# A gated attention and mixture block: batch 1's keys ahead of its transposes, an earlier table load, and a fourth weight base summed early

## The chip, the cores and the metric

The kernel runs on one core of a Trainium2 chip. The metric is the device time of one execution in microseconds (us), as the median of several runs. A core has five engines that each work through a program of their own in order: TensorE (PE, with its weight loads shown apart as PEld), VectorE (DVE), ScalarE (ACT), GpSimd (POOL) and SyncE (SP). They wait for each other by semaphores. SP, ACT and POOL also issue DMAs, and an issue stands in the engine's program like any other instruction.

## The reference

Eight batches of 256 tokens of width 512, all in float32. Cut to what matters:

```python
def attend(x, ctx):                       # x normed; 32 query heads, 8 key heads of 16
    q = heads(concat(ctx, x) @ Wq)
    k = concat(rep(heads(ctx @ Wsk)), rep(heads(x @ Wk)))     # along the keys
    v = concat(rep(heads(ctx @ Wsv)), rep(heads(x @ Wv)))
    s = q @ k.T / 4 + alibi               # only the last 64 positions of each half are seen
    return softmax(s) @ v @ Wo

def ffn(x):                               # x normed
    p4, i4 = top_k(softmax(x @ w_router), 4)
    basis = silu(x @ w_gate) * (x @ w_up)                     # 8 bases of 256 columns
    mixed = sum over the 4 of p4/sum(p4) * scale[i4] * mix[i4] over the bases
    return mixed @ w_down + (silu(x @ sg) * (x @ su)) @ sd    # a shared part of 512

x = x + tanh(g_xattn) * attend(layernorm(x), ctx)
x = x + tanh(g_ffn) * ffn(layernorm(x))
```

## The kernel before

Tokens are handled in two tiles of 128. Each batch b passes through four generators: `project(b)` (norm, transposes, keys, queries, values), `attention(b)` (scores, softmax, value products), two `tail(b, t)` (out-projection, residual, second norm, router) and `feed_forward(b)`.

**Order by hand.** The program runs under a manual schedule: what the Python code emits first stands first on its engine. `run` (L1212) holds the live generators with a virtual time each and always steps the one that is earliest; a generator yields a number of units, and its `start` call says how long all its units are in batches (one batch is about 117 us). So a yield moves no instruction by itself. It decides what is written between two instructions.

**The prologue.** Batch 0's inputs and the attention weights are loaded by SP and ACT (L127 to L145). 14 transposes of an identity (`WARM`, L169) keep PE busy until data arrive. `project_first` (L374) computes batch 0's keys of the context, the transposes of tile 0, the first half of four query groups (the half over the context), then tile 1's transposes, tile 0's keys and the second halves. ACT's first computing instruction (L168) brings in its table; it stands behind all of ACT's load issues.

**The first softmax.** `first_batch` (L728) goes through 19 steps u. A step softens one block of 4 head pairs on DVE (L641), takes exponentials on ACT (L660), divides the block before on POOL (L672) and transposes the one before that on DVE (L685); every second step has new scores on PE (L628), and steps 6, 10, 14 and 18 have value products on PE (L707). Between these, `piece` lets the generator `rest` go on by one slot: a yield of BEFORE or MORE means that the next slot is PE work, AFTER that it is an eviction. `rest` (L437) does batch 0's values, tile 1's keys and queries, and then all of `project(1)`: transposes of tile 0, of tile 1 (L531), the context keys and the keys (L543), four query groups in two halves each (L562), the values (L582). What is left when the steps are over goes on in `others` (L486).

**PSUM banks.** Four banks hold scores, one has the tag "one", three are the gate banks gu0 to gu2. `own` in `rest` takes gu2 and "one" in turn, beginning with gu2; all of `project(1)` is in "one", so each product there waits until the one before has been evicted.

**The bases.** The feed-forward uses sums of weight quarters. The first time that a base k (0 to 9, two of them shared) is used, four sums (`sub`, L947, L953) are made in place and stored to scratch in DRAM (`keep`, L955, L957); later batches load them. `first_weights` (L269) does this for bases 2, 0 and 1 during the first softmax, with all sums on POOL; its loads stand on SP. From base 3 on, `feed_forward(0)` makes the sums of base k during piece k - 1, two on DVE and two on POOL, and stores them between that piece's end and piece k (L1095 to L1133). Each quarter has two buffers, so base k + 2 is loaded when piece k is done with its own (`after`, L357); a base that is already summed (`summed`) takes two loads where another takes one, for three of its four quarters.

**Attention's other parts.** `diagonals` (L491) copies batch values into block form with 16 DMAs per batch, on SP for batches from 1 on.

Of the kernel before, what the change touches and what calls it, by code (L numbers as in the profile page):

```python
# [15 lines left out]
P = 128  # L16
# [14 lines left out]
NSI = SI // P  # L31
LN_EPS, EPS = 1e-5, 1e-8
MASKED = 1e32
WARM = 14


@with_exitstack
def gated_block(
# [44 lines left out]
    def next_bank(name):  # L83
        turns[0] += 1
        return ps_gu.tile([P, 2, T], F32, tag=f"gu{turns[0] % 3}", name=name)
# [24 lines left out]
    def load(b, eng=nc.sync):  # L110
        xt = three.tile([P, NT, HID], F32, tag="x", name=f"x_{b}")
        eng.dma_start(xt, x[b].rearrange("(t p) d -> p t d", p=P))
        return xt
# [7 lines left out]
    def weight(src, rows, cols, name, eng):  # L121
        t = const.tile([P, rows // P, cols], F32, tag=name, name=name)
        eng.dma_start(t, src.rearrange("(c p) n -> p c n", p=P))
        return t
# [8 lines left out]
    def load_queries(half):  # L133
        nc.scalar.dma_start(
            wq_sb[:, half * NC : (half + 1) * NC, :],
            wq[half * HID : (half + 1) * HID].rearrange("(c p) n -> p c n", p=P),
        )
# [1 line left out]
    load_queries(0)  # L139
    wk_sb = weight(wk, HID, HK * D, "wk", nc.scalar)  # L140
    nc.scalar.dma_start(x_0[:, 1, :], x[0, P:, :])
    load_queries(1)
    wsv_sb = weight(wsv, HID, HK * D, "wsv", nc.scalar)
    wv_sb = weight(wv, HID, HK * D, "wv", nc.scalar)
    loaded[1] = load(1, nc.scalar), load_context(1, nc.scalar)  # L145

    ident = const.tile([P, P], F32, tag="ident", name="ident")
    make_identity(nc, ident)
# [17 lines left out]

    warm = const.tile([P, 1], F32, tag="warm", name="warm")
    nc.scalar.activation(warm, neghalf[:, :1], AF.Tanh)  # L168
    idle = next_bank("idle")  # L169
    for _ in range(WARM):  # L170
        nc.tensor.transpose(idle[:, 0, :P], ident, ident)
# [96 lines left out]

    def first_weights():  # L269

        for k in (2, 0, 1):
            for g in range(1, 5):
                load_gu(k, g)
            if k == 2:
                yield 2.0
                later["wd"] = weight(w_down, I, HID, "wd", nc.sync)


                later["sd"] = sd = const.tile([P, NSI // 2, HID], F32, tag="sd", name="sd")
                nc.sync.dma_start(  # L280
                    sd, sw_down.rearrange("(j o p) n -> o p j n", o=2, p=P)[1]
                )
            if k == 0:
                yield 5.5
                yield from first_sums(2)
        yield 1.0
        yield from first_sums(0)
        yield 1.0
        yield from first_sums(1)
# [84 lines left out]
    def project_first():  # L374

        xt, ctT = loaded[0]
        xnT = two.tile([P, NC, T], F32, tag="xo", name="xnT_0")
        kT = two.tile([P, 2, 2, T], F32, tag="kT", name="kT_0")
        qT = two.tile([P, NB, G, Q], F32, tag="qT", name="qT_0")
        tiles = [slice(t * P, (t + 1) * P) for t in range(NT)]  # L380

        def early(name, parts):
            bank = ps_sc.tile([P, 512], F32, tag="sc", name=name)
            return bank.rearrange("p (a n) -> p a n", a=parts)

# [13 lines left out]

        def queries(pq, g, cols, cs):  # L400
            for c in cs:
                nc.tensor.matmul(  # L402
                    pq, lhsT=wq_sb[:, c, g * P : (g + 1) * P],
                    rhs=(ctT if c < NC else xnT)[:, c % NC, cols],
                    start=(c == 0), stop=(c == 2 * NC - 1),
                )

        def put_queries(pq, g, t):
            blocks = slice(t * NB // NT, (t + 1) * NB // NT)
            nc.scalar.activation(  # L410
                qT[:, blocks, g, :], pq.rearrange("p (b q) -> p b q", q=Q), AF.Copy, scale=-0.25
            )

        def two_tiles(shape, name):
            return next_bank(name).rearrange("p t (a n) -> p (t a) n", n=P)

        pk = early("pk_0", 2)
        keys(pk, 0, slice(0, T))
        evict = transposed(xnT, first_normed[0], 0, "x0", lambda shape, name: early(name, NC))
        pqs = [next_bank(f"pq_0_{g}")[:, 0, :P] for g in range(G - 1)]  # L420
        pqs.append(ps_one.tile([P, P], F32, tag="one", name="pq_0_3"))
        for g in range(G):
            queries(pqs[g], g, tiles[0], range(NC))
        put_keys(pk, 0, slice(0, T))
        evict()
        evict = transposed(xnT, first_normed[1], 1, "x0", lambda shape, name: early(name, NC))
        keys(pk, 1, tiles[0])
        for g in range(G):
            queries(pqs[g], g, tiles[0], range(NC, 2 * NC))
        put_keys(pk, 1, tiles[0])  # L430
        evict()
        for g in range(G):
            put_queries(pqs[g], g, 0)
        projected[0] = kT, qT


        def rest():  # L437
            banks = [0]

            def own(name):  # L440
                banks[0] += 1
                if banks[0] % 2:
                    return other_bank(2, name)
                return ps_one.tile([P, 2 * T], F32, tag="one", name=name)

            pv = own("pv_0").rearrange("p (t s n) -> p t s n", t=NT, s=2)
            for t in range(NT):
                yield BEFORE if t == 0 else MORE
                for s, (w_sb, src) in enumerate(((wsv_sb, ctT), (wv_sb, xnT))):
                    for c in range(NC):  # L450
                        nc.tensor.matmul(
                            pv[:, t, s, :], lhsT=src[:, c, tiles[t]], rhs=w_sb[:, c, :],
                            start=(c == 0), stop=(c == NC - 1),
                        )
            yield AFTER
            put_values(pv)
            for qd, eng in enumerate((nc.sync, nc.gpsimd, nc.sync, nc.gpsimd)):
                diagonals(qd, eng)
            yield BEFORE
            pk = own("pk_0_1").rearrange("p (s n) -> p s n", s=2)  # L460
            keys(pk, 1, tiles[1])
            yield AFTER
            put_keys(pk, 1, tiles[1])
            normed = norm(loaded[1][0], range(NT), "a1")
            for g in range(G):
                yield BEFORE
                pq = own(f"pq_0_{g}_1")[:, :P]
                queries(pq, g, tiles[1], range(2 * NC))
                yield AFTER
                put_queries(pq, g, 1)  # L470
                if g == 1:
                    xns = normed()
            ready.add("queries")
            yield from project(1, xns)

        fill.append(rest())
        fill.append(next(fill[0]))
# [29 lines left out]
    def project(b, xns=None):  # L507
# [16 lines left out]
            xns = normed()  # L524
            yield 3.0
        xnT = two.tile([P, NC, T], F32, tag="xo", name=f"xnT_{b}")
        if b == 1:
            yield BEFORE
        for t in range(NT):
            yield from own()  # L530
            evict = transposed(xnT, xns[t], t, f"x{b}", bank)  # L531
            yield AFTER
            evict()
            free()
            yield BEFORE


        kT = two.tile([P, 2, 2, T], F32, tag="kT", name=f"kT_{b}")
        yield from own()
        pk = bank([P, 2, T], f"pk_{b}")  # L540
        for s, (w_sb, src) in enumerate(((wsk_sb, ctT), (wk_sb, xnT))):
            for c in range(NC):
                nc.tensor.matmul(  # L543
                    pk[:, s, :], lhsT=w_sb[:, c, :], rhs=src[:, c, :],
                    start=(c == 0), stop=(c == NC - 1),
                )
            yield AFTER if s else MORE
        for par in range(2):
            for s in range(2):
                nc.scalar.activation(  # L550
# [1 line left out]
                )  # L552
        free()
        yield BEFORE


        qT = two.tile([P, NB, G, Q], F32, tag="qT", name=f"qT_{b}")
# [414 lines left out]
    def feed_forward(b):  # L972
# [120 lines left out]


        for k in range(PIECES):  # L1095
            late = b == 0 and k > 2
            more = b == 0 and 2 < k + 1 < PIECES
            if k == NK:
                shT = one.tile([P, NSI, T], F32, tag="shT", name=f"shT_{b}")
            one_and_five(k)  # L1100
# [125 lines left out]
    project_first()  # L1226
    start(attention(0), 0.38, at=-0.585, total=70.0)
    start(after_diagonals(), 0.2, at=-0.535, total=1.0)
    start(first_weights(), 0.39, at=-0.537, total=20.5)
    start(attention(1), 0.86, at=FIRST, total=74.1)  # L1230
    at = -0.2
    while 0 not in sides:
# [52 lines left out]
```

## Time and profile before

| | |
|---|---|
| runs | 1024.79, 1022.11, 1021.71 us |
| median | 1022.11 us |
| profiled execution | 1024.93 us, of which the span of its instructions 1023.2 us |
| mean granted TensorE clock | 0.991 |
| busy: PE, PEld, DVE, ACT, POOL | 988.1, 797.4, 602.4, 443.5, 470.7 us |
| first score product of batch 0 | 18.49 us |
| first gate product of batch 0 (L1001) | 97.04 us |
| DMA | 192.15 MB, mean 188 GB/s |

The profile is of one execution. Times in it are counted from the start of the span. An engine is busy while it computes; the issue of DMAs is not counted. Where an engine stood idle, the trace names what ended the idle time. "DMA share" is the mean busy share of the core's 16 DMA engines; the granted clock is that of TensorE as a share of full speed.

### The profile page before, as it was taken

How to read it: one execution, taken by the hardware profiler on the slowest of the kernel's cores; microseconds unless marked ns; L12 is line 12 of the kernel's file. 1: busy time of each engine (PE TensorE's matmuls, PEld its weight loads, DVE VectorE, ACT ScalarE, POOL GpSimd, SP SyncE). 2: the span in 40 equal slices, each digit the busy share in tenths (PEclk: the TensorE clock that was granted, in tenths of full speed). 3: DMA queues.
4: the chain of work that ended last, by engine and by line, in shares of the span. 5: the costliest groups of instructions: out<-in, count | busy, mean ns of one | idle time of the engine just before them, and what ended most of it. 6: DMA issues, size and time to landing. Idle time of an engine off the chain costs nothing.

```text
span 1023.2 us, 27845 instructions
## 1 busy us (share of the span) xinstructions
PE 988.1 (97%) x10470; PEld 797.4 (78%) x10470; DVE 602.4 (59%) x2241; ACT 443.5 (43%) x1657; POOL 470.7 (46%) x892
## 2 busy tenths in 40 slices
PE   8788799899999999999999999999999999999998
PEld 8666687777888788886778868787787868786885
DVE  2664766667563775536755377545766466765453
ACT  3653553336542464425643255433654245442231
POOL 4763676635543265423634236432455335651341
PEclk9899899999999999999999999999999999999999
DMA  6933754479444793547844586445954468664891
GB/s 209 246 125 96 235 163 148 156 214 293 155 144 145 198 306 124 165 147 209 268 145 146 166 220 235 136 155 178 279 183 138 145 189 258 202 196 158 270 308 60
DMA packets 117302, 192.15 MB, mean 188 GB/s; under 512 B 12848, under 2 KB 34864, under 8 KB 117168
## 3 DMA queue, kind: packets, MB, share of 16 engines
q1 hardware_dynamic: 112672, 184.87, 58.3%
q10 hardware_dynamic: 4112, 4.46, 1.3%
q8 instruction: 83, 1.36, 0.5%
q0 software_dynamic: 384, 1.05, 0.5%
q14 instruction: 51, 0.42, 0.1%
HBM read 158.87 MB, written 14.68 MB: 170 GB/s over the span
## 4 chain that ended last, share of the span: by engine, by line
PE 82%; DVE 9%; issue 3%; ACT 3%; POOL 2%; DMA 1%; SPq 1%; ACTq 0%; DVEq 0%; POOLq 0%
PE m L1001 34%; PE m L1010 10%; PE pq L562 8%; PE sc L707 6%; PE po L866 5%; PE sc L628 4%; PE pd L1144 4%; PE pk L543 3%; PE pv L582 2%; PE pd L1147 2%; DVE pr L641 1%; ACT pr L660 1%; PE pq L402 1%; PE pl L896 1%; DVE th L968 1%
## 5 line engine op out<-in xcount | busy, mean ns | idle before, releaser
L672 POOL TENSOR_SCALAR pr<-pr,rd 128x192 f32<-128x192 f32 (+2 forms) x512 | 211.1, 430 | 250.2 <-DVE rd L669 231.6
L660 ACT ACTIVATE pr<-pr,nm 128x192 f32<-128x192 f32 (+2 forms) x512 | 220.0, 433 | 112.6 <-DVE nm L641 59.9
L1001 PE MATMUL m<-w,sT 128*128 128x256 f32 x1024 | 252.5, 380 | 0.9 <-issue 0.6
L1001 PEld LDWEIGHTS m<-w,sT 128*128 128x128 f32 x1024 | 193.7, 190 | 28.8 <-issue 1.5
L641 DVE CUSTOM_DVE_ANT_1 pr<-sc,nbias 128x192 f32<-128x192 f32 (+2 forms) x512 | 154.0, 322 | 101.6 <-PE sc L628 95.4
L1001 PE MATMUL m<-w,hT 128*128 128x256 f32 x768 | 203.9, 388 | 1.0 <-DVE u L1046 1.0
L1001 PEld LDWEIGHTS m<-w,hT 128*128 128x128 f32 x768 | 139.6, 191 | 25.6 <-issue 6.5
L1091 POOL TENSOR_TENSOR mixed<-mixed,th 128x256 f32<-128x256 f32 x112 | 81.3, 726 | 139.3 <-DVE th L1086 139.3
L685 DVE STREAM_TRANSPOSE pt<-pr 128x768 f32<-128x768 f32 (+2 forms) x128 | 111.5, 871 | 4.6 <-POOL pr L672 3.1
L660 ACT ACTIVATION_READ_ACCUMULATOR pr<-pr,nm 128x1 f32 x512 | 98.5, 192 | 0.0
L1047 POOL TENSOR_TENSOR m<-m,u 128x256 f32<-128x256 f32 x80 | 61.3, 766 | 69.1 <-DVE u L1046 60.2
L963 ACT ACTIVATE th<-m 128x256 f32<-128x256 f32 x80 | 30.8, 385 | 138.3 <-DVE up L1057 138.2
L707 PEld LDWEIGHTS sc<-pt,vbd 64*32 64x32 f32 x5120 | 61.3, 107 | 26.1 <-issue 14.1
L707 PE MATMUL sc<-pt,vbd 64*32 64x64 f32 (+2 forms) x5120 | 69.1, 230 | 9.0 <-DVE nm L641 5.2
L1069 DVE TENSOR_TENSOR gate<-u,m 128x256 f32<-128x256 f32 x80 | 33.3, 416 | 70.1 <-PE m L1001 66.3
L1057 DVE TENSOR_TENSOR up<-u,m 128x256 f32<-128x256 f32 x80 | 33.3, 417 | 67.9 <-PE m L1001 41.0
L628 PE MATMUL sc<-kT,qT 32*128 32x192 f32 (+2 forms) x1024 | 64.6, 337 | 4.6 <-DVE nm L641 4.2
L628 PEld LDWEIGHTS sc<-kT,qT 32*128 32x128 f32 x1024 | 44.8, 185 | 28.7 <-issue 8.9
L963 ACT ACTIVATE th<-gate 128x256 f32<-128x256 f32 x80 | 33.2, 416 | 76.4 <-DVE gate L1069 76.4
L1010 PE MATMUL m<-sT,w 128*128 128x128 f32 x512 | 66.0, 278 | 0.0
L1010 PEld LDWEIGHTS m<-sT,w 128*128 128x128 f32 x512 | 62.3, 194 | 0.4
L1144 PE MATMUL pd<-sd,shT 128*128 128x512 f32 x128 | 61.5, 603 | 0.1
(131 smaller groups left out, 1375.9 us busy)
## 6 DMA issues: line engine op xcount, KB each, us to landing
w<-s SPq DMA_DIRECT2D x284, 256.0 KB, 3.5
w<-in_L_ffn_w_gate SPq DMA_DIRECT2D x130, 256.0 KB, 3.0
w<-in_L_ffn_w_up SPq DMA_DIRECT2D x73, 256.0 KB, 4.1
vbd<-vpad SPq DMA_DIRECT2D x120, 128.0 KB, 3.0
s<-w SPq DMA_DIRECT2D x40, 256.0 KB, 3.2
w<-in_L_ffn_shared_w_gate SPq DMA_DIRECT2D x32, 256.0 KB, 2.7
w<-in_L_ffn_shared_w_up SPq DMA_DIRECT2D x18, 256.0 KB, 3.8
sd<-in_L_ffn_shared_w_down SPq DMA_DIRECT2D x16, 256.0 KB, 3.5
```

What stands on the lines that cost most here:

```text
L562: nc.tensor.matmul(pq, lhsT=wq_sb[:, c, g * P : (g + 1) * P], rhs=(ctT if c < NC else xnT)[:, c % NC, :], start=(c == 0), stop=(c == 2 * N ...
L628: nc.tensor.matmul(seen(scs[p][:, j * COLS : (j + 1) * COLS], qb), lhsT=qT[rows, qb].rearrange("p g q -> p (g q)"), rhs=kT[rows, par, :, f ...
L641: nc.vector.tensor_tensor_reduce(out=part, in0=seen(scs[p][:, j * COLS : (j + 1) * COLS], qb0 + j), in1=bass.AP(tensor=bias.tensor, offset ...
L660: nc.scalar.activation(part, part, AF.Exp, bias=nmax, scale=-1.0, accum_out=den)
L672: nc.gpsimd.tensor_scalar(part, part, rden[:, p : p + 1], 1.0, op0=ALU.mult, op1=ALU.mult)
L685: nc.vector.transpose(pt[:, u % 4].rearrange("p c (s k) -> p (c s) k", s=2)[:, :, lo:], pr.rearrange("p c (s k) -> p (c s) k", s=2)[:, :, ...
L707: nc.tensor.matmul(scs[gp][32 * c : 32 * (c + 1), 2 * COLS + lo * Q : 2 * COLS + hi * Q], lhsT=vbd[rows, kb % (P // Q), kb // (P // Q) * 2 ...
L963: nc.scalar.activation(th, gate, AF.Tanh, scale=0.5)
L1001: nc.tensor.matmul(dst, lhsT=sides_of[m][c], rhs=w[:, c, :], start=(first and c == 0), stop=(c == NC // 2 - 1), skip_group_check=True,)
L1010: nc.tensor.matmul(dst[:, cols], lhsT=w[:, c, cols], rhs=sides_of[m][c], start=(first and ic == c == 0), stop=(c == NC // 2 - 1), skip_gro ...
L1091: nc.gpsimd.tensor_add(mixed[t], mixed[t], th)
L1144: nc.tensor.matmul(po, lhsT=shT[:, ic, t * P : (t + 1) * P], rhs=down[ic], **flags)
```

## The change

- `WARM` is 20 instead of 14.
- ACT's table load comes ahead of the loads of the second half of wq, of wsv and of wv; batch 1's inputs are loaded by ACT after the first eviction of transposes.
- In `project_first` tile 0's transposes stand between the second and the third query group.
- `own` in `rest` begins with "one".
- `project(1)` does the context keys first (in "one"), then both transposes (in gu2), then the other keys, and has one empty slot ahead of its queries. From batch 2 on, 1.0 unit is added after each eviction of transposes.
- `first_weights` handles bases 2, 3, 0, 1. Base 3's sums follow base 2's; bases 0 and 1 are loaded after that. Its length and units go from 0.39 and 20.5 to 0.40 and 25.5. `feed_forward(0)` makes sums only for bases from 4 on.

```diff
-WARM = 14
+WARM = 20
...
     nc.scalar.dma_start(x_0[:, 1, :], x[0, P:, :])
-    load_queries(1)
-    wsv_sb = weight(wsv, HID, HK * D, "wsv", nc.scalar)
-    wv_sb = weight(wv, HID, HK * D, "wv", nc.scalar)
-    loaded[1] = load(1, nc.scalar), load_context(1, nc.scalar)
...
     nc.scalar.activation(warm, neghalf[:, :1], AF.Tanh)
+    load_queries(1)
+    wsv_sb = weight(wsv, HID, HK * D, "wsv", nc.scalar)
+    wv_sb = weight(wv, HID, HK * D, "wv", nc.scalar)
...
-        for k in (2, 0, 1):
+        for k in (2, 3, 0, 1):
             for g in range(1, 5):
                 load_gu(k, g)
...
-            if k == 0:
+            if k == 3:
                 yield 5.5
                 yield from first_sums(2)
+                yield 1.0
+                yield from first_sums(3)
...
-        evict = transposed(xnT, first_normed[0], 0, "x0", lambda shape, name: early(name, NC))
         for g in range(G):
+            if g == G // 2:
+                evict = transposed(
+                    xnT, first_normed[0], 0, "x0", lambda shape, name: early(name, NC)
+                )
             queries(pqs[g], g, tiles[0], range(NC))
         put_keys(pk, 0, slice(0, T))
         evict()
+        loaded[1] = load(1, nc.scalar), load_context(1, nc.scalar)
...
-                if banks[0] % 2:
+                if banks[0] % 2 == 0:
                     return other_bank(2, name)
...
+        if b == 1:
+
+            yield BEFORE
+            yield from own()
+            pk = bank([P, 2, T], f"pk_{b}")
+            keys(pk, 0)
+            for t in range(NT):
+                yield MORE
+                evict = transposed(
+                    xnT, xns[t], t, f"x{b}",
+                    lambda shape, name: other_bank(2, name).rearrange("p (c n) -> p c n", n=P),
+                )
+                yield AFTER
+                evict()
+            yield BEFORE
+            keys(pk, 1)
+            yield AFTER
+        else:
+            for t in range(NT):
+                yield from own()
+                evict = transposed(xnT, xns[t], t, f"x{b}", bank)
+                yield AFTER
+                evict()
+                free()
+                yield BEFORE + 1.0
...
         free()
         yield BEFORE
+        if b == 1:
+            yield BEFORE
...
-            late = b == 0 and k > 2
-            more = b == 0 and 2 < k + 1 < PIECES
+            late = b == 0 and k > 3
+            more = b == 0 and 3 < k + 1 < PIECES
...
-    start(first_weights(), 0.39, at=-0.537, total=20.5)
+    start(first_weights(), 0.40, at=-0.537, total=25.5)
```

More of the change, by code (lines that the diff above doesn't have):

```diff
@@ L526, in project, with keys @@
         xnT = two.tile([P, NC, T], F32, tag="xo", name=f"xnT_{b}")
[L527 to L535, printed above, removed]
         kT = two.tile([P, 2, 2, T], F32, tag="kT", name=f"kT_{b}")
-        yield from own()
-        pk = bank([P, 2, T], f"pk_{b}")
-        for s, (w_sb, src) in enumerate(((wsk_sb, ctT), (wk_sb, xnT))):
+        def keys(pk, s):
+            w_sb, src = ((wsk_sb, ctT), (wk_sb, xnT))[s]
             for c in range(NC):
@@ L546, in project @@
                 )
-            yield AFTER if s else MORE
+        if b == 1:
[22 more added lines that the diff above has]
+                yield BEFORE + 1.0
+            yield from own()
+            pk = bank([P, 2, T], f"pk_{b}")
+            for s in range(2):
+                keys(pk, s)
+                yield AFTER
         for par in range(2):
```

## The prediction

> **What bounds the kernel now.** I read the page first: the busy times and the chain of work that ended last.
>
> ```profile
> PE 988.1 (97%) x10470; PEld 797.4 (78%) x10470; DVE 602.4 (59%) x2241; ACT 443.5 (43%) x1657; POOL 470.7 (46%) x892
> PE 82%; DVE 9%; issue 3%; ACT 3%; POOL 2%; DMA 1%; SPq 1%; ACTq 0%; DVEq 0%; POOLq 0%
> ```
>
> TensorE (PE) is busy for 988 of 1023.2 us, so time is to be won only where PE stands idle or runs at a lowered clock. The busy time by stretches of time says where (columns: length, busy us and instructions of PE, weight load, DVE, ACT, POOL, then granted clock, DMA share, GB/s).
>
> ```profile
> 41.28:57.50 16.22, 11.90 (x193) 9.05 (x193) 9.40 (x46) 12.25 (x50) 12.16 (x22) 0.89 0.90 264
> 57.50:97.04 39.54, 35.58 (x565) 26.12 (x564) 22.04 (x84) 14.95 (x58) 20.30 (x34) 1.00 0.24 79
> 97.04:119.80 22.76, 22.43 (x197) 17.75 (x195) 15.63 (x79) 13.93 (x58) 12.86 (x30) 1.00 0.93 263
> 119.80:130.00 10.20, 4.96 (x76) 4.26 (x77) 9.72 (x31) 3.30 (x13) 7.25 (x8) 0.67 0.39 127
> 317.00:434.00 117.00, 116.22 (x1188) 93.93 (x1185) 69.99 (x266) 54.02 (x203) 51.64 (x102) 1.00 0.60 188
> ```
>
> A steady batch (last line) has 0.8 us idle in 117. The losses lie in batch 1's projection beside batch 0's softmax (41 to 57), and in one hole at 120. What PE waited for, by time, in the first 130 us:
>
> ```profile
> PE sc L707 <- DVE nm L641: 5.2, 1, 5.2
> PE sc L628 <- DVE nm L641: 2.3, 2, 1.7
> PE pq L562 <- ACT kT L550: 1.7, 1, 1.7
> PE pk L543 <- ACT xnT L205: 1.6, 1, 1.6
> ```
>
> The chain in order of time says what is behind the first of them:
>
> ```profile
> 114.17 5.80 DMA w<-in_L_ffn_w_up
> 119.97 0.02 issue
> 119.99 0.69 DVE w L953
> ...
> 124.63 0.35 DVE pr L641
> 124.97 0.02 DVE nm L641
> 124.99 0.04 issue
> 125.04 1.55 PE sc L707 x47
> ```
>
> L953 is the first weight sum of base 3. It stands in DVE's program in piece 2, reads a load issued at 114.17 that landed at 119.97, and held DVE idle for 3.12 us. Behind it DVE needed 5 us to reach the softening that PE's value products wait for. So PE stood from 119.79 to 125.04.
>
> **The clock, from the same rows.** By windows of 3.41 us the granted clock is 0.50 in 36.28 to 39.70, 46.50 to 49.90 and 121.6 to 128.4. The windows ahead of these had PE busy for 1.59, 1.11 and 1.27 us; after 1.74 busy (53.30 to 56.70) the clock stayed at 1.00. So a wait of some 1.8 us in a window costs the next one half its speed: the context keys at 46.12 took 3.44 us, the other keys 1.99 (lost 1.45); after 125.04 two rows took 2.06 and 1.55 where the same forms took 1.03 and 1.05 (lost 1.5). The Trainium skill, "TensorE: Matmul & The Clock Gate", section "Part 1: The HAM clock gate (the "warmup" mystery)", gives the same 3.4 us window, but has the clock fall after an idle window. By that rule none of the waits of 2 us would cost clock, and 1.45 us less would be won; the rows decide for half-idle windows.
>
> **The parts.**
>
> A. *Prologue.* The 14 idle transposes run 1.37 to 4.62 (0.232 us each); PE then stands 0.92 us until the context and its key weight land at 5.54. The eight key products take 3.67 us against 1.99 elsewhere. Six more transposes (1.4 us) close the hole; the keys then end at 7.6 to 9.7 instead of 9.2. The queries that now follow need the first half of wq, issued 1.27, landed 7.7 later: 8.97. Before, they started at 9.48 behind the first transposes (0.44), which now stand between the second and third query group (0.9 us each) at about 11.3; normed data was ready at 8.60. The second half of wq, issued at 4.6 instead of 3.12, queues behind 1.8 MB of the same queue at 370 GB/s and landed at 13.2; it is needed at 14.3. ScalarE's table load (1.28) starts at 3.1 instead of 9.78, so the first eviction is no longer behind it. Batch 1's loads (issue 1.85 and 0.48) now stand in ACT's program behind the first eviction (11.9) and ahead of the second key eviction (14.59): 12.5 + 2.3 = 14.8 at worst. They landed 9.0 and 8.5 after issue: by 23.3 at the latest, needed at 25.5 (norm) and 41.3 (context). Gain 0.2 us, bounds -0.5 (keys stay slow and start at 6.0) to 0.5.
>
> B. *Batch 1's projection.* Keys of the context (needing no norm) go first, in bank "one"; the transposes take the third gate bank. Gone: the transposes' waits of 0.37 and 0.70, the keys' wait of 1.59 with its 1.45 of clock, and the query wait of 1.66 for the key eviction (the slot after it is now empty, and the out-projection, 3.43, and scores come in between): 5.8 us. The projection ends one slot later: half a query group and the values move behind the out-projection of tile 1 (po). There PE now waits 1.30 for the normed tile and 0.68 for its eviction (94.71, 96.04); two value pieces of 2 us each fill that. In all 7.8 us. Batch 1's attention is written out only once its queries are, some 0.027 of a batch (3 us) later against batch 0's feed-forward than before, and its diagonal copies with it; its value products come 20 us behind those copies, so nothing waits.
>
> What is late next: ACT was busy for all of 43.10 to 46.50, so the first transposes' eviction comes at about 45.2 to 45.8 and the second transposes wait some 1.5; scores wait 0.45. On POOL the sums of base 2 come a slot earlier, and two of them (1.27 each) now precede the division that ran at 45.10: it ends at 48.7 instead of 46.73, the DVE transpose behind it (0.97) at 49.7, and the value products start there: 2.1 us idle, and a window of low clock (1.5). I take 2.0 and half of the last 3.6: 3.8. Gain 7.8 - 3.8 = 4.0; bounds 1.0 and 7.8.
>
> Base 3's four sums add 4 x 1.27 = 5.1 us to POOL before 82 us, where it has 5.9 us of holes at 58.5 to 62.83 and 73.14 to 74.71 alone. SP issues four more loads and four more stores (0.33 to 0.45 each, 3 us) in 62 to 94, where it only waited for POOL. Bases 0 and 1 are now loaded after base 3's last store; a load landed in 3.0 to 4.4, and the first sum of base 0 stands one division (1.63) and one softmax step (3 to 4) later: 0 to 1.5 of POOL time.
>
> The Trainium skill, "SBUF — State Buffer", section "SBUF: two separate sides", speaks against sums on POOL: DVE's two-port operations and POOL lock each other out for a whole instruction. The norm's product at 93.18, beside two sums, took 1.48 where 0.54 is usual; beside the softening no such loss shows. By the rule each of base 3's four sums could cost DVE 1.27; by the row one 0.9, in a stretch where DVE is 56% busy.
>
> C. *The hole at 120.* With base 3 stored already, piece 2 has no sums: DVE loses the 3.12 wait, 0.69 and 0.95; POOL 2.80. Value products would start at about 120.5, so 4.5 of 5.25 go, and the clock's 1.5: 6.0. Against it: base 3 is now loaded with its sums, seven loads instead of four, three more of 256 KB at 370 GB/s (0.7 each), in a stretch whose DMA share is 0.93, behind 16 diagonal copies (0.6 each on SP). One of them is ahead of base 2's last load, which PE already waited 0.31 for; that stretch cannot start earlier than the values' eviction. I charge 1.5. Base 4's sums become the first late ones; their load moves from 116.4 to 118, the need from 125 on. Gain 4.5; bounds 0 (hole moves to base 4) and 6.8.
>
> D. *Batches 2 to 7.* Each transposes' step is given 1.0 unit more of the written order (0.62 of a batch's 117 us over 60 units: 1.2 us). Five waits of 0.46 us for ACT's eviction (2.3) can go; no row shows what comes instead, so from +2.3 lost to 2.3 won; I take 1.0 won, since other PE work stands ready there.
>
> **Sum.** 0.2 + 4.0 + 4.5 + 1.0 = 9.7 us. The profiled execution took 1024.93 (span 1023.2 and 1.7 around it): 1015.2 by its own time. The median of the three runs is 2.8 lower, 1022.11: 1012.4.
>
> **Rivals.**
> 1. *The hole moves on*: PE or base 4's sum waits for the extra loads, C gives 0. For it: DMA share 0.93 and SP without pause. Against: base 4's sums stand a whole piece (7 us, from 103.69 to 110.67) further on. 1022.1 - 5.2 = 1017.
> 2. *POOL paces the softmax*: B gives about 0 where POOL's 5.1 us are not hidden. For: it is 75% busy in 41 to 57. Against: the holes named above. 1022.1 - 5.7 = 1016.4.
> 3. *Slower*: POOL stands for base 0's load. It can be issued only behind base 3's last store, and POOL has it in front of the division of score block 14. Each us beyond the 1.5 of slack is added to the softmax; four stores and three loads are 1.8 MB, 5 us at 370 GB/s, and 2 of latency; twice (bases 0 and 1) 11 us. From 8 us of standing on, B is negative, and with the hole moved as well the time is 1026. Against: DMA share 0.24 in 57 to 97.
> 4. *Nothing*: the waits removed in B and C return as others, 1020 to 1024.
>
> **How the numbers follow.** Forecast 0.60 (1012.4, its own range 1007 to 1017); rival 1 0.12; rival 2 0.10; rival 4 0.10; rival 3 0.08. About 0.3% (3.1 us) is what a measurement of this kernel can tell from no change. Faster: 0.60 + 0.12 + 0.10 = 0.82; within: 0.10; slower: 0.08. With all terms at their good ends the time would be 1005; 5 in 100 lie below 1007, 15 above 1020.
>
> **What would show it.** The keys at 5.5 to 6 take 2 us (A); in 41 to 60 PE's waits fall below 3 us and the score products of block 6 start before 59 instead of at 61.05; the first gate product of batch 0 starts at 92 to 94 instead of 97.04 (B); no DVE wait for a load and no PE hole over 2 us in 110 to 130 (C); fewer PE waits for the evicted transposes after 200 (D). Wrong: a PE or DVE wait for a weight load of base 2, 3 or 4; POOL idle with a load as its releaser; steady batches above 117.5 us.

## The result, and the profile after

| | before | after |
|---|---|---|
| median us (lowest to highest, runs) | 1023.38 (1021.57 to 1030.98, 14) | 1031.07 (1029.86 to 1036.77, 14) |
| profiled execution, its span | 1024.93, 1023.2 | 1036.77, 1035.0 |
| mean granted clock | 0.991 | 0.985 |

The ratio is 1.0072, 95% interval 1.0057 to 1.0088: the change made the kernel 7.4 us slower. The forecast was 9.7 us faster.

The page of the changed kernel, busy times and the shares of the chain by engine:

```profile
PE 991.6 (96%) x10476; PEld 800.9 (77%) x10476; DVE 598.2 (58%) x2239; ACT 439.8 (42%) x1657; POOL 470.2 (45%) x894
PE 88%; DMA 4%; DVE 4%; SPq 2%; issue 1%; POOL 1%; ACT 1%; ACTq 0%; DVEq 0%; POOLq 0%
```

The profiled execution of the changed kernel is the slowest of its 14, 5.7 us above their median; so its span differs from before by more than the medians do. PE is busy 3.5 us longer than before, but the span grew by 11.8: the rest is idle time of PE. On the chain, DMA went from 1 to 4%. The same stretches as in the prediction (columns as there):

```profile
41.28:57.50 16.22, 13.10 (x204) 8.88 (x203) 10.48 (x49) 11.13 (x45) 14.39 (x26) 0.89 0.94 287
...
97.04:119.80 22.76, 16.33 (x101) 13.35 (x99) 15.59 (x71) 12.03 (x53) 13.56 (x29) 0.93 0.91 240
...
317.00:434.00 117.00, 114.80 (x1172) 92.17 (x1171) 69.77 (x271) 52.95 (x201) 49.96 (x100) 0.99 0.60 183
```

PE is 1.2 us busier in 41 to 57.5, as forecast. In 97 to 120 it lost 6.1, and a steady batch now has 2.2 us idle in 117 instead of 0.8. What PE waited for in the whole execution:

```profile
PE pq L589 <- DVE x L898: 11.0, 5, 2.2
PE m L1028 <- DMA w<-in_L_ffn_w_up: 9.4, 1, 9.4
```

(Columns: total us, how many, the longest. Lines are about 27 further on than in the kernel before: L589 query groups, L898 residual sum, L893 out-projection, L655 scores, L668 softening, L1028 gate products, L501 diagonal copies.) Both are new. The second is one of the signs that the prediction named for its being wrong; the first is nowhere in it, and comes once in each of five batch periods. First the second, a hole. The chain in order of time:

```profile
106.46 10.40 DMA vbd<-vpad
...
117.56 5.14 DMA w<-in_L_ffn_w_up
...
122.74 2.08 PE m L1028 x4
```

PE stands from 113.4 to 122.74 for the last quarter of base 2, and the chain goes back through SP's issues and a diagonal copy. SP's own rows (start, length of the issues, count at the end), after:

```profile
104.84 0.43 SPq L112 DMA_DIRECT2D x<-in_x  x1
...
105.82 4.08 SPq L501 DMA_DIRECT2D vbd<-vpad  x4
...
113.32 4.19 SPq L501 DMA_DIRECT2D vbd<-vpad  x4
117.56 0.59 SPq L350 DMA_DIRECT2D w<-in_L_ffn_w_up  x1
```

and before:

```profile
107.42 2.89 SPq L496 DMA_DIRECT2D vbd<-vpad  x4
110.37 1.68 SPq L112 DMA_DIRECT2D x<-in_x  x1
...
113.16 0.43 SPq L349 DMA_DIRECT2D w<-in_L_ffn_w_up  x1
```

Before, the last of the four diagonal groups was issued at 107.42, then batch 2's inputs (x and the context), then base 2's last quarter at 113.16. After, the last two groups stand behind the inputs, each behind one more quarter load (the third behind the one at 103.74, the fourth behind that at 110.01), and the quarter left 4.4 us later. SP's waits until batch 2's inputs had landed take 3.6 us there (last section). PE came to the quarter earlier as well. Before, its row there was

```profile
118.66 1.13 PE L1001 MATMUL m<-w,sT 128*128 128x256 f32 x4 [0.31 <-DMA w<-in_L_ffn_w_up]
```

Counted from the first gate product (97.04 before, 94.55 after), the quarter was issued at 16.1 us before and at 23.0 after, and PE was ready for it at 21.3 before and at 18.8 after. So 6.9 us of the longer wait are the later issue, and 2.5 us are PE's earlier coming (the transfer itself took 0.3 us less).

The batches by the first store of each: before 235.06, 357.86, 479.62, 602.64, 725.21, 847.49; after 230.68, 358.87, 482.80, 609.49, 733.57, 859.26. The first comes 4.4 us earlier, in spite of the hole; then the five batches take 16.2 us more.

**How far one profile carries.** Up to 97 us the changed kernel and its variant `fix_00` (below) have the same written order on PE, yet their first gate products are at 94.55 and 98.88 (granted clock from 18.4 us to there 0.96 and 0.92). So the 2.5 us by which that product moved from before (97.04) show nothing; gains there are judged by medians.

### The profile page after: what moved, and what is told of

Read it like the earlier page. It is cut to its first block, busy times and chain, and to the rows that moved or that the text cites. A ratio compares the mean times of both kernels' runs of the same rounds, so it can differ in the third digit from the quotient of the medians.

```text
span 1035.0 us, 27837 instructions
## 1 busy us (share of the span) xinstructions
PE 991.6 (96%) x10476; PEld 800.9 (77%) x10476; DVE 598.2 (58%) x2239; ACT 439.8 (42%) x1657; POOL 470.2 (45%) x894
## 4 chain that ended last, share of the span: by engine, by line
PE 88%; DMA 4%; DVE 4%; SPq 2%; issue 1%; POOL 1%; ACT 1%; ACTq 0%; DVEq 0%; POOLq 0%
PE m L1028 37%; PE m L1037 10%; PE pq L589 9%; PE sc L734 6%; PE pd L1171 5%; PE po L893 5%; PE sc L655 5%; PE pd L1174 2%; PE pv L609 2%; PE pk L537 2%; PE pl L923 1%; DMA vbd<-vpad 1%; DMA w<-in_L_ffn_w_up 1%; SPq L501 1%; DMA wo<-in_L_xattn_Wo 1%
## 5 line engine op out<-in xcount | busy, mean ns | idle before, releaser
L1028 PE MATMUL m<-w,sT 128*128 128x256 f32 x1024 | 253.0, 381 | 9.4 <-DMA w<-in_L_ffn_w_up 9.4
L1028 PEld LDWEIGHTS m<-w,sT 128*128 128x128 f32 x1024 | 194.6, 191 | 36.8 <-DMA w<-in_L_ffn_w_up 9.8
L668 DVE CUSTOM_DVE_ANT_1 pr<-sc,nbias 128x192 f32<-128x192 f32 (+2 forms) x512 | 153.7, 322 | 98.2 <-PE sc L655 97.2
L1028 PE MATMUL m<-w,hT 128*128 128x256 f32 x768 | 205.0, 390 | 2.4 <-issue 1.3
L1028 PEld LDWEIGHTS m<-w,hT 128*128 128x128 f32 x768 | 141.2, 192 | 26.2 <-issue 6.1
L734 PE MATMUL sc<-pt,vbd 64*32 64x96 f32 (+2 forms) x5120 | 69.6, 231 | 4.6 <-DVE pt L712 1.6
L655 PE MATMUL sc<-kT,qT 32*128 32x192 f32 (+2 forms) x1024 | 65.1, 339 | 5.6 <-DVE nm L668 5.3
L589 PE MATMUL pq<-ctT,wq 128*128 128x256 f32 x224 | 58.4, 407 | 11.0 <-DVE x L898 11.0
L1060 ACT COPY u<-m 128x256 f32<-128x256 f32 x80 | 29.5, 369 | 92.6 <-PE m L1028 64.1
L655 PEld LDWEIGHTS sc<-kT,qT 32*128 32x128 f32 x1024 | 45.5, 186 | 29.4 <-DVE nm L668 8.0
L1075 POOL TENSOR_TENSOR m<-m,m 128x256 f32<-128x256 f32 x80 | 58.7, 734 | 6.3
```

What stands on the lines that cost most here:

```text
L589: nc.tensor.matmul(pq, lhsT=wq_sb[:, c, g * P : (g + 1) * P], rhs=(ctT if c < NC else xnT)[:, c % NC, :], start=(c == 0), stop=(c == 2 * N ...
L655: nc.tensor.matmul(seen(scs[p][:, j * COLS : (j + 1) * COLS], qb), lhsT=qT[rows, qb].rearrange("p g q -> p (g q)"), rhs=kT[rows, par, :, f ...
L668: nc.vector.tensor_tensor_reduce(out=part, in0=seen(scs[p][:, j * COLS : (j + 1) * COLS], qb0 + j), in1=bass.AP(tensor=bias.tensor, offset ...
L734: nc.tensor.matmul(scs[gp][32 * c : 32 * (c + 1), 2 * COLS + lo * Q : 2 * COLS + hi * Q], lhsT=vbd[rows, kb % (P // Q), kb // (P // Q) * 2 ...
L1028: nc.tensor.matmul(dst, lhsT=sides_of[m][c], rhs=w[:, c, :], start=(first and c == 0), stop=(c == NC // 2 - 1), skip_group_check=True,)
L1075: nc.gpsimd.tensor_add(m7, m7, tiles.pop(("m5", k)))
```

## The experiments

Each kernel is named by its label. A ratio is to the kernel before, timed beside it. The tail (`tail`) is the generator that writes the out-projection po, the residual sum and the second norm. Theory T1 at the outset: the added unit alone makes the loss, because the first query group now stands two gate blocks behind po, needs its bank, and waits for the residual sum. T3, S, V and S2 are explained where they come up.

### Which part: the added unit

`no_unit`, the changed kernel with the unit taken out:

```diff
-                yield BEFORE + 1.0
+                yield BEFORE
```

> The changed kernel without the added unit in batches 2 to 7. Theory 1 (the unit writes the out-projection of tile 0 ahead of the first query group, and the queries then wait in PE for bank one): the five waits of 2.2 us and the low clock behind them go, batches take 122 to 123 us again between their stores, and the time is 1016 to 1020 us. Theory 2 (batches 1 to 6 are slower because batch 1's attention starts later, and the delay is handed on): 1029 to 1032 us, the batches as slow as in the changed kernel.

1026.61 us, ratio 1.0020 (1.0007 to 1.0033). The waits for the residual sum are gone and the batches take 121 to 125 us; a wait of 8.9 for w_up stays. So there are two faults: one in the unit, one in the rest.

`unit_only`, the kernel before with the unit alone:

```diff
-            yield BEFORE
+            yield BEFORE + (0.0 if b == 1 else 1.0)
```

> The kernel before with nothing but the added unit. Theory 1: PE waits of about 2 us for the residual sum in five or six batches, 1032 to 1038 us. Theory 2: within 2 us of the kernel before.

1032.23 us, ratio 1.0072 (1.0057 to 1.0087), with the same five waits of 2.2: the unit alone costs as much as the whole change.

`unit_04`, the same with 0.4 for 1.0:

> The kernel before with 0.4 unit added instead of 1.0: as written out, the first query group still stands ahead of the out-projection, and other products stand between the two transposes. Theory 1 (the order of the holders of bank one decides): no wait for the residual sum, the 0.46 us waits for the evicted transposes gone, 1019 to 1022.5 us. Rival (each delay of the projection costs in proportion): 0.4 of what the whole unit costs, 1026 to 1029 us.

1022.28 us, ratio 0.9975 (0.9963 to 0.9986). One wait for a residual sum (3.8 us, in batch 0) and none later; the transposes' waits are gone. Not four tenths of the loss but a gain: what counts is in which order the unit lets things be written.

`unit_gap`, `unit_only` with the first query group held back, so that more gate blocks stand between po and it:

```diff
         for g in range(G):
-            yield from own()
+            yield from hold(0.0 if b == 1 else 0.06 if g == 0 else GAP)
```

> The kernel before with the whole unit, and with the first query group held back 0.06 of a batch after the out-projection has given bank one back: the out-projection still comes first, but the queries are written behind a block of value products. Theory 1 (PE loses by having the query in its queue ahead of the residual sum): no PE wait for the residual sum, 1018 to 1026 us. Rival (the out-projection ahead of the queries is itself the loss, by what it does to DVE): still 1030 us or more.

1036.89 us, ratio 1.0112 (1.0089 to 1.0135). The wait for the residual sum is gone, and another of the same kind is there:

```profile
PE m L1001 <- DVE th L968: 9.7, 5, 1.9
```

T1 falls, in its time too: the query group was not the cause, only the first to ask DVE for something.

### Why: what DVE does during the out-projection

The changed kernel's PE rows of batch 2's projection, written order "po, scores, two gate blocks, query group" (in the kernel before, the query group and the scores stood ahead of po):

```profile
271.59 3.60 PE L893 MATMUL po<-wo,oT 128*128 128x512 f32 x8
275.12 0.93 PE L655 MATMUL sc<-kT,qT 32*128 32x192 f32 x16
...
280.18 3.68 PE L589 MATMUL pq<-ctT,wq 128*128 128x256 f32 x8 [2.20 <-DVE x L898]
```

the same place before:

```profile
272.02 1.89 PE L562 MATMUL pq<-ctT,wq 128*128 128x256 f32 x8
...
278.16 0.93 PE L628 MATMUL sc<-kT,qT 32*128 32x192 f32 x16
...
280.85 3.60 PE L866 MATMUL po<-wo,oT 128*128 128x512 f32 x8
```

and the changed kernel's DVE:

```profile
276.07 0.36 DVE L668 CUSTOM_DVE_ANT_1 pr<-sc,nbias 128x192 f32<-128x192 f32 x1 [5.58 <-PE sc L655]
...
279.37 0.75 DVE L898 SCALAR_TENSOR_TENSOR x<-po,tg,x 128x512 f32<-128x512 f32 x1
```

DVE is idle for 5.58 us, over the end of a gate block, po and the scores: po gives it nothing until it ends. Then the scores' softenings, a transpose and gate work, all written ahead of the residual sum, come at once: 3.3 us of it stand ahead of L898. The query group's bank is free only behind it. That is T3: **po must not stand ahead of the score block**. `unit_po_26`, `unit_only` with po later by 0.6 of the tail's units, just behind the scores:

```diff
 def tail(b, t, oT):
-        yield 2.0
+        yield 2.0 if b == 0 or t == 1 else 2.6
```

> The kernel before with the added unit in batches 2 to 7 (the variant that came out at 1032.2) and one edit more: the first tile's attention tail of batches 1 to 7 starts 0.6 of its units later, so that the written order of TensorE's work reads 'scores, output projection, two gate blocks, first query group' instead of 'output projection, scores, two gate blocks, first query group'. Theory T3 (the output projection stands ahead of a score block, so VectorE has nothing for 3.6 us, and then its softenings come ahead of the residual sum for which the query group's bank waits): the five waits of 2.2 us of the first query group for the residual sum are gone, batch periods 120 to 123 us, 1020 to 1025 us in all. Rival (what counts is only that the projection's bank is wanted again two gate blocks later, wherever the scores stand): five waits of 1.5 us or more stay, 1028 us or more.

1015.58 us, ratio 0.9915 (0.9898 to 0.9931): by the ratios 16 us less than `unit_only`, and 8.7 less than before. T3 holds as the cause of the unit's loss, and more was won than it had said. The later tail without the unit was not run, so the 8.7 us belong to the pair; how much of it is the unit's is open. Its PE and DVE rows at the same place (the scores are at 271.47):

```profile
272.33 3.70 PE L866 MATMUL po<-wo,oT 128*128 128x512 f32 x8
...
277.60 1.89 PE L562 MATMUL pq<-ctT,wq 128*128 128x256 f32 x8
```

```profile
272.42 0.36 DVE L641 CUSTOM_DVE_ANT_1 pr<-sc,nbias 128x192 f32<-128x192 f32 x1 [2.15 <-PE sc L628]
...
276.07 0.75 DVE L871 SCALAR_TENSOR_TENSOR x<-po,tg,x 128x512 f32<-128x512 f32 x1 [0.27 <-PE po L866]
```

The softenings run while po runs; DVE is free 0.27 us before po ends, and the query group, again two gate blocks behind po, starts without a wait.

### The hole: loads or their order

Theory S: batch 2's input loads, now ahead of two diagonal groups on SP, make the hole. Rival V: the extra loads' volume does. `base3_only`, the kernel before with only `first_weights` and the bounds in `feed_forward(0)` changed:

```diff
-        for k in (2, 0, 1):
+        for k in (2, 3, 0, 1):
```

> The kernel before with base 3's loads and sum ahead of base 0's alone. On SP the four diagonal groups of batch 1 still stand ahead of batch 2's input loads, as in the kernel before. Theory S (the hole near 120 us in the changed kernel is made by batch 2's two input loads standing ahead of two diagonal groups, whose end the value products and so the next quarter's load wait for): the hole of 5.25 us at 120 us is gone and no other of over 2 us is in its place, 1016 to 1021 us. Rival V (four more quarter loads before 90 us are what delays a later quarter, whatever the order): a hole of 5 us or more stays, 1023 us or more.

1020.62 us, ratio 0.9959 (0.9944 to 0.9974): 4.2 us won, against the 4.5 of the prediction's C. Where the hole was, PE's only waits are

```profile
120.78 1.13 PE L1003 MATMUL m<-w,sT 128*128 128x256 f32 x4 [0.33 <-DMA w<-in_L_ffn_w_up]
122.47 1.15 PE L709 MATMUL sc<-pt,vbd 64*32 64x96 f32 x64 [0.56 <-DVE nm L643]
```

The seven loads fit. `no_unit_no_base3` has the prologue and batch 1's keys first, without base 3 and the unit:

> The changed kernel without the added unit and without base 3: the prologue and batch 1's keys first. Batch 2's input loads stand ahead of two of batch 1's diagonal groups on SP, as in the changed kernel. Theory S: a wait of TensorE for a quarter of a w_up or a sum of base 3 stays between 110 and 130 us, 5 us or longer; first gate product about 2 us earlier than before; 1020 to 1025 us. Rival V: without the extra loads the hole is no longer than before's 5.25 us, so that the 2 to 4 us won ahead of it stay: 1017 to 1020 us.

1022.48 us, ratio 0.9978 (0.9966 to 0.9990). A wait of 6.8 for w_up is there without any extra load. V falls as the source, and batch 1's part brings the hole (the prologue alone leaves a wait of 1.46 there). Base 3 adds to it: with base 3 (`no_unit`) the wait is 8.9, and the kernel is 4.3 us slower by the ratios (1.0020 against 0.9978), where base 3 by itself won 4.2. In these two profiles the first gate product is at 96.06 and 91.68, so a part of the loss may lie ahead of the hole; its cause is open. `no_unit_x2_late` moves batch 2's inputs behind all diagonals and three quarter loads:

```diff
+            if b == 2:
+                yield 5.0
             loaded[b] = load(b), load_context(b)
-            yield 16.0
+            yield 16.0 - (5.0 if b == 2 else 0.0)
```

> The changed kernel without the added unit (1026.6), with batch 2's two input loads issued 5 units of their process later: on SP they stand behind all four of batch 1's diagonal groups and three quarter loads. Theory S: TensorE's wait of 8.9 us for base 2's last quarter near 115 us is gone or under 2 us, first store of batch 0 at 226 to 229 us, 1013 to 1019 us in all. Rival V: the wait stays at 5 us or more, over 1022 us.

1026.91 us, ratio 1.0019 (1.0000 to 1.0037), a miss for both. The wait for w_up fell to 3.1, but the chain now reads

```profile
116.29 5.45 DMA x<-in_x
...
121.76 0.70 DVE st_a L178
```

Batch 2's statistics stand in DVE's program ahead of softenings; with x late DVE stood for it, and PE for DVE (2.7). `fix_00` and `fix_20` are both the changed kernel with the tail's 2.6; `fix_20` has 2.0 for the 5.0 above as well.

> The changed kernel whole, with one edit: the first tile's attention tail of batches 1 to 7 starts 0.6 of its units later, so that its output projection is written behind a score block instead of ahead of it. T3: the waits of the query groups for the residual sum go as they did without the other parts (16.6 us there), 1013 to 1018 us; the wait of some 9 us for a w_up quarter near 115 us stays. Rival (the changed kernel's loss has another source beside the unit's): 1022 us or more.

> The changed kernel with the tail 0.6 of its units later and batch 2's two input loads 2 units later: on SP they stand behind all four of batch 1's diagonal groups, but, unlike in the try with 5 units, ahead of the next quarter loads, as in the kernel with base 3 alone. Theory S: no wait for a quarter of w_up of over 2 us between 100 and 130 us and no late softening behind batch 2's statistics; 6 to 9 us faster than the same kernel without the later inputs: 1005 to 1011 us. Rival V (the volume of the loads counts, not their order): a wait of 5 us or more stays, within 3 us of that kernel.

1018.28 us, ratio 0.9947 (0.9929 to 0.9965), and 1017.12, 0.9937 (0.9923 to 0.9950). T3 holds in the whole kernel too (12.8 us less than the changed kernel, with the wait of 9.4 still in it). S fails as the whole cause: 6.5 of the 9.4 us stay. What `fix_20` keeps is that the diagonals stand one quarter load later. That is S2: SP issues in order, and the quarter's load is behind the diagonals (16 copies took 10.7 us of SP before and 13.8 after, pauses within a group included). `hoist_0` issues the four groups two and two (first excerpt), `dact_0` the last two on ACT's queue (second excerpt). Both are on `fix_00`:

```diff
-                if u in (1, 2) and step < 2:
+                if b == 1 and u == 1 and step < 2:
+                    diagonals(2 * step, nc.sync)
+                    diagonals(2 * step + 1, nc.sync)
+                elif b != 1 and u in (1, 2) and step < 2:
                     diagonals(2 * (u - 1) + step, nc.sync)
```

```diff
                 if u in (1, 2) and step < 2:
-                    diagonals(2 * (u - 1) + step, nc.sync)
+                    diagonals(2 * (u - 1) + step, nc.scalar if b == 1 and u == 2 else nc.sync)
```

> The changed kernel with the tail 0.6 of its units later (1018.3, with a wait of 9.4 us) and batch 1's four diagonal groups issued two and two in its second softmax unit, instead of one and one in its second and third. On SP no diagonal group then stands between the last quarters' loads and batch 2's inputs stand behind all of them. Theory S2 (SP issues in order, and the late groups hold the quarter's load back): the wait goes from 9.4 to under 3 us, 1009 to 1013 us. Rival V (the transfers themselves): 6 us or more stay, over 1015 us.

> The changed kernel with the tail 0.6 of its units later and batch 1's third and fourth diagonal groups issued on ScalarE's queue at the place where SP issued them. The same transfers at about the same time, eight fewer issues on SP. Theory S2: the wait of 9.4 us falls under 4 us, 1010 to 1015 us; rival V: 6 us or more stay. ScalarE has 12 of 23 us busy there, so its eight issues may cost 1 or 2 us elsewhere.

`hoist_0` 1016.76, ratio 0.9929 (0.9910 to 0.9947): the wait fell to 4.5, and one of 1.7 for a stored sum came: short of S2's 3 us, and not the rival's 6. `dact_0` 1014.57, 0.9914 (0.9892 to 0.9936): with the same transfers and eight fewer issues on SP, PE no longer waits for a load there; its longest wait is now for ACT, which does the issuing:

```profile
PE m L1028 <- ACT m L1061: 3.3, 1, 3.3
```

So the same transfers need not make the hole. The run does not say by itself that SP's issuing made it: the last two groups were also issued earlier (102 to 110 us instead of 110 to 122 in `fix_00`), batch 2's inputs stood behind them, and PE, having stood 3.3 us for ACT, came to the quarter later. The written order names one statement that put the groups there: the empty slot behind batch 1's keys. `end_0` is `fix_00` without it:

```diff
         yield BEFORE
-        if b == 1:
-            yield BEFORE
```

> The changed kernel with the tail 0.6 of its units later (1018.28, wait of 9.4 us) and without the second unit of 0.8 behind batch 1's keys. On SP the four diagonal groups and batch 2's inputs then stand in the order of the kernel before, one quarter load earlier than in the changed kernel. Theory S2: the wait for the quarter of w_up is under 2 us, 8 to 11 us less in all: 1007 to 1011 us. Rival (TensorE comes to that quarter too early whatever the order, since batch 1's projection is shorter): a wait of 4 us or more stays, 1013 us or more.

1013.13 us, ratio 0.9893 (0.9871 to 0.9915). PE waits 0.38 for that quarter, and SP's rows have the order of the kernel before again:

```profile
110.23 2.74 SPq L501 DMA_DIRECT2D vbd<-vpad  x4
113.02 1.29 SPq L112 DMA_DIRECT2D x<-in_x  x1
...
115.90 0.43 SPq L350 DMA_DIRECT2D w<-in_L_ffn_w_up  x1
```

S2 holds: counted from the first gate product, the quarter is issued at 17.1 us instead of 22.9 in `fix_00`. The rival has a part in it: without the slot PE is ready for the quarter only at 22.2 us instead of 18.8. That part of the wait is moved and not won; in time the edit was worth 5.5 us by the ratios, not the expected 8 to 11.

### What the prologue and batch 1's projection are worth

`prologue_only`, the kernel before with the prologue's edits:

> The kernel before with the prologue's edits alone: the table ahead of some of ScalarE's loads, batch 1's x and context loaded later, the first transposes between the second and the third query group, 20 warming transposes. Reading of the changed kernel's trace (keys of batch 0 sooner, its first scores at 18.70 instead of 18.49 us): nothing is won or lost, within 1.5 us of the kernel before. Rival (batch 1's inputs come late and its norms with them): 2 us or more slower, with a wait of TensorE for batch 1's normalised x between 30 and 60 us.

1025.17 us, ratio 1.0018 (1.0004 to 1.0032): nothing won, 1.8 lost. `best1` leaves out the prologue and batch 1's part: the kernel before with base 3, the unit and the tail's 2.6.

> The kernel before with three edits: base 3 beside the first softmax, the added unit in batches 2 to 7, the first tile's tail 0.6 of its units later. The hole's 4.2 us (base 3 alone) and the 9 us of the unit with the later tail add up: 1008 to 1014 us. Rival (both move the same wait, since the hole lies in batch 0, where the later query groups fell too): 1014 to 1018 us.

1012.35 us, ratio 0.9894 (0.9877 to 0.9911), the same as `end_0`, which has both parts (batch 1's without its empty slot). `best2` is `best1` with the diagonals two and two, `nopro_hoist_0` is `hoist_0` with the old prologue, `nopro_end_0` is `end_0` with the old prologue.

> The kernel before with base 3 beside the first softmax, the added unit, the tail 0.6 later (1012.35 without more) and batch 1's four diagonal groups two and two. No wait for a quarter load was left there, so nothing or up to 1 us is won: 1011 to 1013 us. Against nopro_hoist_0 batch 1's projection is the one difference: if its 2 to 4 us are real, nopro_hoist_0 is faster by that; if they are lost again behind (POOL's sums, softmax), the two agree within 1.5 us.

> As hoist_0 but with the prologue of the kernel before. The prologue alone was 1.8 us slower than the kernel before, so 1 to 3 us less than hoist_0: 1007 to 1012 us. Rival (the prologue's loss was its own collision with the hole near 120 us, which is gone here): the same as hoist_0 within 1 us.

> The same with the prologue of the kernel before: batch 1's keys first, base 3, the unit, the tail later. Within 1.5 us of the kernel with the new prologue, since the two prologues were equal within 1 us where the diagonals were hoisted. Against the kernel before with base 3, the unit and the later tail (1012.35) batch 1's projection is the one difference: 2 to 4 us faster than that if its gain holds, the same if POOL's sums or the loads take it back.

`best2` 1014.22, 0.9902 (0.9885 to 0.9920); `nopro_hoist_0` 1017.35, 0.9943 (0.9922 to 0.9964); `nopro_end_0` 1014.99, 0.9913 (0.9892 to 0.9935). Batch 1's projection, the one difference in two pairs, is worth nothing (`nopro_end_0` beside `best1`) or less (`nopro_hoist_0` beside `best2`); the 2 to 4 us expected of it did not come. The prologue makes no difference that these pairs can tell. The best versions, `best1` and `end_0`, beat both given kernels: about 11 us less than before, 18 less than after.

## Why the prediction was wrong

**D failed, and decided the sign.** It put the unit at 1.0 us won within 2.3 either way, "since other PE work stands ready there". The unit alone cost 7.4 us (5.8 to 8.9 by its interval). The bounds were made from the waits that the unit could remove, not from what it moves: it moves everything written in the same stretch against each other, and put po ahead of a score block. Waits of 2.2 in five batches are 11.0 us, and some of the query products behind them ran at a lowered clock. With po behind the scores the unit and the later tail together won 8.7 us. The cost was not to be read in any row of before, but its ingredients were: po 3.60, the softenings, and an in-order DVE that needs both.

**C's size was right, its place was not safe.** By itself base 3 won 4.2 us (4.5 forecast). The charge of 1.5 for extra loads was not seen (0.33 and 0.56 of waits stay). But a cost came that the sum does not have: in `base3_only` POOL stood 3.2 us for a quarter load, and PE waited 1.24 us at 81.8 for DVE, which it did not before. That forecast and measurement agree so closely is in part luck. In the whole change it met a hole from B, the one that rival 1 has in kind ("the hole moves on") but ascribes to base 3's loads: `base3_only` has no such hole, and `no_unit_no_base3` has it without those loads (6.8 us, 8.9 with them).

**B failed at "its diagonal copies with it; its value products come 20 us behind those copies, so nothing waits".** The value products do not wait, but SP's own next issue does: the last quarter of base 2 stands behind the copies in SP's program. The step followed a DMA to its reader and not to what is queued behind its issue. The same slot that removed the query group's wait of 1.66 moved the copies; in `end_0`, without it, that wait is back:

```profile
PE pq L587 <- ACT kT L575: 1.7, 1, 1.7
```

So are the 1.30 and 0.68 us beside po that B had counted as filled.

The keys' wait of 1.6 is gone there, but the two that B had named as late next came: the transposes for an eviction, 1.5, and the value products for DVE's transpose, 1.6 (2.1 forecast, half of it charged). The 4.0 forecast is 0 by `end_0` and `best1`.

**A** was put at 0.2 won, and 1.8 were lost by the median of `prologue_only` (0.4 to 3.3). Its steps came: the keys took 1.99 there, the queries waited 1.44 for wq. But the first scores started at 18.68 (18.49 before); the 0.2 us of the trace explain a part of the loss at most. PE's wait for base 2's last quarter is 1.46 there (0.31 before); whether that is the rest was not tested.

**Rivals.** Rival 3, the slower one, named POOL. POOL stood twice for quarter loads in 22 to 100, 2.9 and 0.9 us (never before the change): the mechanism is there, far from its 8 us, and `base3_only`, with 3.2, won all the same. A slower case through a written order was not among the rivals, and so slower had 0.08.

**The sum, by runs.** Base 3 alone is -4.2 and the unit with the later tail -8.7, in sum -12.9; together (`best1`) they are -10.8, and where the other 2 went was not traced. In the changed kernel stand against this po ahead of the scores (12.8, after to `fix_00`) and the slot behind batch 1's keys (5.5, `fix_00` to `end_0`): 18.3 us of written order against 11.0 of gains (`end_0`), a net loss of 7.3 us.

**The clock.** The prediction's reading that a wait of some 1.8 us in a window halves the next one's clock does not hold as a rule (last section).

## What to carry to other kernels

Where a schedule writes several streams into in-order engines, a pause in one stream is a reordering of all of them: price it by writing out the new order at each place that it reaches, and ask of each long product which engine it leaves without work and who needs that engine next. A moved DMA is to be followed twice, to its reader and to the instruction behind its issue on the same queue. A change that bundles four edits can hide two good ones: here two of them, with one number changed (2.0 to 2.6), were worth 1.1%.

## What the runs showed of the hardware

- **The clock can fall after a window that is only part idle.** In the changed kernel PE was busy 1.03 of 3.23 us around a wait of 2.20; the next 3.68 us were granted 0.54, and eight products took 3.68 instead of 1.99:

```profile
276.95:280.18 3.23, 1.03 (x6) 0.58 (x4) 3.20 (x11) 0.69 (x4) 3.15 (x7) 1.00 0.48 162
280.18:283.86 3.68, 3.68 (x9) 2.96 (x10) 3.16 (x12) 1.80 (x7) 1.55 (x4) 0.54 0.00 0
```

  The length of the wait does not decide it: in `unit_only` three of the five waits of 2.20 were followed by products of 1.99. Nor does PE's busy time in a window of 3.41 us: after 1.55 us (655.7 to 659.1 of the changed kernel) the clock stayed at 1.00, after 2.12 us (44.77 to 48.18) it fell to 0.50. What decides is open. The Trainium skill, "TensorE: Matmul & The Clock Gate", section "Part 1: The HAM clock gate (the "warmup" mystery)", has the clock fall after an idle window; these rows do not need a whole one.
- **An issue can wait for a transfer that it does not use.** Two of SP's issues of diagonals waited for batch 2's inputs, issued eight issues earlier and landing 8.4 and 10.1 us after their issue (60 to 125 us of the changed kernel; SP's waits):

```profile
SPq L501 <- DMA x<-in_x: 2.1, 1, 2.1
SPq L501 <- DMA ctT<-in_ctx: 1.5, 1, 1.5
```

  In `fix_20` the inputs stand behind the diagonals, neither wait is there ahead of the quarter's issue, and PE's wait for the quarter is 2.9 us shorter.
- **Two executions of the same order on PE can differ by 4.3 us in the first 97 us** (94.55 and 98.88 above).
